# Four graph layers on one core: layer 2's first block moved ahead of W1, the residual row's store and load moved to the end of k, a smaller count for the weight ring, and VectorE in GpSimd's place for the deep weight sums

## The chip, the core and the metric

The kernel runs on one core of a Trainium2 chip. The metric is device time in microseconds (us), the median over runs of the same program. Before the change it is 2749.14 us, the median of three runs that span 2746.19 to 2756.6 us. One execution was profiled: it took 2744.72 us, and the span of its profile, from the first to the last instruction, is 2742.9 us.

The engines are named as the profile names them: PE is the matrix engine (TensorE), PEld its weight load, DVE is VectorE, ACT is ScalarE, POOL is GpSimd, SP is SyncE, which issues most transfers here. A queue is the in-order list of instructions of one engine.

## The reference, cut to what matters

The input is x of shape (128, 64, 512) in float32, that is 8192 rows of 512, with 128 graphs of 64 nodes and an adjacency matrix `adj` (64 x 64) for each. Four layers follow each other, each with a residual and a layer norm:

```
x = _layernorm(x + _L0_gnn_ref(x, adj, L0_gnn_W1, ...), axis=-1)     # relu(S x W1 + b1), norm, S h W2 + b2, + x
x = _layernorm(x + _L1_gnn_ref(x, adj, L1_gnn_w, L1_gnn_a), axis=-1) # tanh/exp scores, A x w
x = _layernorm(x + _L2_gnn_ref(x, adj, L2_gnn_W1, ...), axis=-1)     # three times adj (x W) + b, relu between
x = _layernorm(x + _L3_gnn_ref(x, nodemask, adj, adj, L3_gnn_W_qkv, L3_gnn_W_out, L3_gnn_b_out), axis=-1)  # 8 heads
```

S is a normalised incidence product made from `adj` (layer 0); layer 3 is attention over 64 nodes with a mask, to which 0.33 adj and 0.33 exp(-adj) are added after the softmax. All arithmetic is float32.

## The kernel before

**Tiles and groups.** Two graphs make a pair of 128 rows and four pairs a group of 512 rows, `xg`, a tile of 128 x 4 x 512 floats (1 MB). There are 16 groups, each taken through all four layers before its rows are written out. Three such x tiles exist (`xp`, three buffers), so group q's rows can be loaded only when group q - 3's rows have been stored.

**Products.** Every 512 x 512 weight product is made by `multiply` with seven quarter products in place of eight (a Strassen scheme: B11, T1, T2, B21, T3, B22, T4), PE accumulating in PSUM while ACT or DVE take the partial sums out. One quarter product of one left tile takes PE 1.73 us. The q, k and v products of groups 1 to 14 use the scheme twice over (`deep_multiply`): 42 stages of four or three 128 x 128 blocks, 0.89 or 0.67 us each, and the weights for them are sums made once, in group 0's time, and kept in DRAM (`deep_kept`). In these names `wqd`, `wkd`, `wvd` are the deep weight tiles.

**Deep weight sums.** `Weight.make_deep` makes them before the change. For each of w_q, w_k and w_v it takes the four quarters and the sums T1 to T4 that lie in weight ring tiles (`got`), lets POOL make 28 subtractions of 128 x 128 blocks (lines 335 to 338) into two `big` tiles, and stores everything from the POOL queue (lines 339 to 341). It is called from `Weight.making` (line 394), after POOL's own stores of T1 to T4 (line 392).

**The order of the work.** Three groups are in hand at once. In step s group s is in its first half ("a": layers 0 and 1), group s - 1 in its second half up to the scores ("b": layer 2, then q, k, the start of v), group s - 2 in its tail ("t": rest of v, softmax, output product, last norm). Each half is a Python generator that is cut at named points, and the list `order` (line 1905) says which piece is issued next; `step_1` and `step_last` replace it in the first and the last step. A steady step takes 165 to 172 us. In `order`, `t.v1 t.v2 a.c1 t.v a.w1a1 b.gt` means: two pieces of v of the tail group, then `a.c1` (`graph_T`: 128 small 64 x 64 products of x and S), the last of v, the first three quarter products of W1, then `b.gt` (the same kind of 128 small products, with `adj`, ahead of layer 2's first weight). From q to W1's end PE, DVE and ACT get their instructions in exactly this order (`strict`).

**The planner beside it.** Small work of DVE and ACT (norms, softmax, sums) is not at a fixed place: `Side` keeps a clock for PE, DVE and ACT from written-in costs and issues a task's next piece when it would not make its engine late. Tasks have ranks, the lower first. Layer 1's norm (`out_steps`, rank 3) and the last norm of the tail group (`ln3`, rank 2) run in q and k; the tail norm's remaining five pieces are 0.4 us of DVE and four scalings on ACT.

**Queues.** The build orders each queue itself: of the instructions that are ready in its model it takes the one that stands first in the program; `in_turn(E)` and `behind(key)` (both `tc.issue_after`) tie one instruction behind another of the same engine. On the chip an instruction waits only for the data and the buffers that it needs. That the order in SP's queue is not the order of the program shows in the `adn` loads: that of group 5 stands in step 4, before that step's `b.gh` (677.6 us in the trace), and was issued at 539.7 us, because its buffer was free.

**The weight ring.** Weight tiles (256 KB, deep ones 256 or 192 KB) pass through a ring of 16 buffers (`wring`, `RING`). `Stream.pump` writes the next loads into the program as long as the count of tiles held, `held`, stays within `RING`; `done` lowers the count after each product and pumps again.

**x, its store and its adds.** The store of a finished group is issued on SP by the last norm's steps when they are through (`then`, line 619, from line 1687). `load_x` (line 238) is a POOL-queue transfer that stands at `loadx`, after `b.k`, and waits for that store. Two rows are added to x by POOL-queue transfers that accumulate (`add_rows`, line 1075): gb3 from `shifted`, at `b.gh`, and bo after the softmax; the second is held back by a one-column copy on POOL, `due` (line 1667).

Of the kernel before, what the change touches and what calls it, by code (L numbers as in the profile page):

```python
# [8 lines left out]
FP = mybir.dt.float32  # L9
# [5 lines left out]
P = 128  # L15
# [20 lines left out]
B11, B21, B22, T1, T2, T3, T4 = range(7)  # L36
ORDER = (B11, T1, T2, B21, T3, B22, T4)
RING = 16

DEEP = ((B11, B21, T1, T2), (T3, T4, B22))  # L40
STAGES = (B11, B21, B22, T1, T2, T3, T4)
# [14 lines left out]
def kernel(  # L56
# [28 lines left out]
    nc = tc.nc  # L85
# [221 lines left out]
    class Weight:  # L307
# [15 lines left out]
            nc.sync.dma_start(out=t, in_=self.deep_kept[h][:, STAGES.index(s)].rearrange("p r n -> p (r n)"))  # L323
            return t.rearrange("p (r n) -> p r n", r=n)

        def make_deep(self, got):

            self.deep_kept = []
            for h, rs in enumerate(DEEP):
                n = len(rs)  # L330
                k = dram.tile([P, 7, n, P], FP, name=f"{self.name}deep{h}", tag=f"{self.name}deep{h}")
                d = big.tile([P, 4, n, P], FP, name=f"{self.name}deep_{h}", tag="big")
                for i, r in enumerate(rs):
                    b = got[r][0].rearrange("p k (n c) -> p k n c", n=2)
                    nc.gpsimd.tensor_sub(d[:, 0, i], b[:, 0, 1], b[:, 0, 0])
                    nc.gpsimd.tensor_sub(d[:, 1, i], b[:, 1, 1], d[:, 0, i])
                    nc.gpsimd.tensor_sub(d[:, 2, i], b[:, 1, 1], b[:, 0, 1])
                    nc.gpsimd.tensor_sub(d[:, 3, i], b[:, 1, 0], d[:, 1, i])
                    nc.gpsimd.dma_start(out=k[:, 0:2, i], in_=b[:, :, 0])
                    nc.gpsimd.dma_start(out=k[:, 2, i], in_=b[:, 1, 1])  # L340
                nc.gpsimd.dma_start(out=k[:, 3:7], in_=d)
                self.deep_kept.append(k)

        def load(self, q, what, u):
            t = self.tile(f"w{what}", q, u)
# [22 lines left out]
        def making(self, quads):  # L368


            got = [[None] * self.halves for _ in range(7)]
            to_keep = []
            for u, b in enumerate(quads):
                t1, t2, t3, t4 = (self.tile(f"t{n}", 0, u) for n in range(1, 5))
                vec.tensor_sub(t1, b[0, 1], b[0, 0])
                vec.tensor_sub(t2, b[1, 1], t1)
                if self.halves == 1:
                    yield
                vec.tensor_sub(t3, b[1, 1], b[0, 1])
                vec.tensor_sub(t4, b[1, 0], t2)  # L380
                made = {T1: t1, T2: t2, T3: t3, T4: t4}
                whole = {B11: b[0, 0], B21: b[1, 0], B22: b[1, 1]}
                kept = {}
                for what, t in (whole | made if self.scaled else made).items():
                    kept[what] = dram.tile([P, 2, Q], FP, name=f"{self.name}k{what}_{u}", tag=f"{self.name}k{what}_{u}")
                    to_keep.append((kept[what], t))
                self.kept.append(kept)
                for what, t in (whole | made).items():
                    got[what][u] = t
            with in_turn(POOL):  # L390
                for k, t in to_keep:
                    nc.gpsimd.dma_start(out=k, in_=t)
                if self.deep:
                    self.make_deep(got)
            yield got

        def load_raw(self):
# [50 lines left out]
    class Stream:  # L448


        def __init__(self, uses):
            self.todo = []
            for wt, q in uses:
                if wt.deep and 0 < q < NGRP - 1:
                    if wt is w_q:
                        trio = (w_q, w_k, w_v)
                        self.todo += [(trio[i // 2], q, (i % 2, s), 1) for i, s in deep_stages(6)]
                elif q == 0:
                    self.todo.append((wt, q, None, 8))
                elif (wt, q) == (w_o, NGRP - 1):  # L460
                    self.todo.append((wt, q, None, 4))
                else:
                    self.todo += [(wt, q, what, wt.halves) for what in ORDER]
            self.here = {}
            self.held = 0
            self.to_make = {}
            self.uses = uses

        def pump(self, uses=None):
            end = len(self.todo) - uses if uses else 0  # L470
            while len(self.todo) > end and self.held + self.todo[0][3] <= RING:
# [605 lines left out]
    def shifted(g, key):  # L1077

        with behind(key):
            if 0 < g["q"] < NGRP - 1:  # L1080
                add_rows(g["x"], gb3_bc)
            else:
                for p in range(G):
                    vec.tensor_add(g["x"][:, p, :], g["x"][:, p, :], gb3_bc)
            prepare_masks(g)
# [359 lines left out]
    def second_half(g):  # L1445
# [70 lines left out]
                    else:  # L1516
                        act.activation(o[:, :, h, :], cols, AF.Relu, bias=gb2_col[:, k : k + 1])  # L1517
        if not alone:
            shifted(g, f"l0w2_{q + 1}.u2")
        h2.sums()  # L1520
        if q == NGRP - 1:
            last_add["h2s"] = newest(DVE)
# [67 lines left out]
        else:  # L1590
# [1 line left out]
            side.start(1.5)  # L1592
            before = groups[q - 1]
            if "ln3" in before:
                before["ln3"] = side.add(before["ln3"], 2)
            more = side.add(left.more_sums(), 0)
            for _ in range(4):
                side.step(more)
# [63 lines left out]
        yield "soft2"  # L1662
        pts = [turn_probs(g, duo, probs[duo]) for duo in range(2)]
        if 0 < q:
            due = small.tile([P, 1], FP, name=f"due_{q}", tag="due")
            with in_turn(POOL):
                nc.gpsimd.tensor_copy(due, pts[0][0][:, 0, 0:1])
            with in_turn(POOL):
                add_rows(xg, bo_bc)
        yield "ptp"  # L1670
        left = Left(f"oT_{q}")
        taken(0, attend(g, 0, pts[0], v), left)
# [11 lines left out]
        whole(gen)  # L1684
        yield "o"
        o = out[q * T : (q + 1) * T, :].rearrange("(p t) d -> t p d", t=P)
        steps = norm_steps(xg, f"l3_{q}", lambda: nc.sync.dma_start(out=o, in_=xg), f"l2_{q + 1}")
        for _ in range(G + 2):
            next(steps)
        g["ln3"] = steps  # L1690
# [198 lines left out]
    def taken(duo, ps, left, both=False):  # L1889
# [25 lines left out]

    step_last = """
# [44 lines left out]
    with in_turn(SP):  # L1961
        load_adn(first)
        w_2.load_raw()
    scaling, bw_parts = w_2.scale(), w_2.beta_times()
    for n, (who, q, name) in enumerate(todo):
        if n == n_start:
# [113 lines left out]
```

## Time and profile before

| what | value |
|---|---|
| median of 3 runs | 2749.14 us |
| profiled execution, its span | 2744.72 us, 2742.9 us |
| PE busy | 2691.6 us, 98% |
| DVE, ACT, POOL busy | 76%, 45%, 6% |
| mean DMA rate | 183 GB/s |
| steady steps, from the start of one `xtp` transpose to the next (395.1 to 2576.3 us) | 165.4 to 171.6 us |
| store of x: issue to landing | 6.1 to 7.3 us, median 6.5 |
| load of x: issue to landing | 8.5 to 11.0 us, median 9.2 |

PE's idle time is what can be saved: 51 us of the span. The profile names for each wait the engine that ended it, or "issue" when the engine waited for nothing that the profile shows. Windows of the trace give busy time, the granted clock of PE (PEclk, 1.00 is full) and the share of the 16 DMA engines' time that packets took (1.00 and a little over is full).

### The profile page before, as it was taken

To read this page: it belongs to the slowest core of one execution; us is meant where nothing else is said; L and a number is where in the kernel's file an instruction comes from. 1 tells how busy PE (TensorE), PEld (TensorE's weight loads), DVE (VectorE), ACT (ScalarE), POOL (GpSimd) and SP (SyncE) were. 2 spreads that over 40 slices of the span, in tenths; PEclk is the share of its full clock that TensorE was granted. 3 is DMA by queue.
4 is the path that set the end of the run, shared out by engine and by line. 5 is a ranking of instruction groups with operands and counts; after the bars stand their busy time and mean duration, and the time that the engine had idled before them with its cause. 6 is when DMAs were issued, how large, how long until landed. Compare 5 with 4: busy or idle time off the path is not lost.

```text
span 2742.9 us, 74095 instructions
## 1 busy us (share of the span) xinstructions
PE 2691.6 (98%) x30536; PEld 2377.5 (87%) x30536; DVE 2092.4 (76%) x4169; ACT 1231.5 (45%) x2860; POOL 162.6 (6%) x259
## 2 busy tenths in 40 slices
PE   9998999999999999999999999999999999999998
PEld 8887888898898889889898888888988888898887
DVE  6777687686887868778687776877868787786866
ACT  3333335355362634526355363453634536264452
POOL 3019000000000000000000000000000000000000
PEclk9999999999999999999999999999999999999999
DMA  8446657576574756648575575665856658475652
GB/s 270 140 146 226 179 157 229 145 231 159 174 230 136 236 154 209 188 136 254 146 235 154 146 242 142 223 161 147 247 143 227 156 167 236 128 237 156 188 170 77
DMA packets 349518, 502.36 MB, mean 183 GB/s; under 512 B 63344, under 2 KB 196752, under 8 KB 348800
## 3 DMA queue, kind: packets, MB, share of 16 engines
q1 hardware_dynamic: 323072, 428.59, 50.2%
q0 software_dynamic: 25968, 68.92, 10.6%
q8 instruction: 243, 3.98, 0.6%
q14 instruction: 91, 0.75, 0.1%
q10 hardware_dynamic: 144, 0.13, 0.0%
HBM read 427.59 MB, written 40.57 MB: 171 GB/s over the span
## 4 chain that ended last, share of the span: by engine, by line
PE 91%; DVE 5%; ACT 2%; issue 1%; POOL 1%; DMA 0%; DVEq 0%; ACTq 0%; POOLq 0%
PE a_l0w L860 8%; PE a_l0w L145 7%; PE a_l2b L860 4%; PE a_l2c L860 4%; PE b_l0w L860 4%; PE a_wo L860 4%; PE a_v L145 4%; PE b_l0w L145 3%; PE a_l2a L145 3%; PE a_k L145 3%; PE a_q L145 3%; PE a_l1w L860 3%; PE gt_l0h L632 2%; PE gt_l L145 2%; PE c_l0w L860 2%; PE b_l2c L860 2%
## 5 line engine op out<-in xcount | busy, mean ns | idle before, releaser
L860 PE MATMUL a_l0w<-w2w,aT_l0h 128*128 128x256 f32 x720 | 164.3, 381 | 0.0
L860 PEld LDWEIGHTS a_l0w<-w2w,aT_l0h 128*128 128x128 f32 x720 | 135.6, 190 | 18.8
L145 ACT ACTIVATE sm<-sm,mx 128x64 f32<-128x64 f32 x416 | 139.1, 340 | 0.2
L1517 ACT ACTIVATE aT_h<-gth,gb_col 128x256 f32<-128x256 f32 x124 | 47.1, 490 | 159.0 <-PE gth L1505 159.0
L145 ACT COPY aT_l<-gt_l 128x512 f32<-128x512 f32 x124 | 64.4, 596 | 101.4 <-PE gt_l L145 101.4
L860 PE MATMUL b_l0w<-w2w,s_l0h 128*128 128x256 f32 x480 | 108.5, 379 | 0.0
L145 PE MATMUL a_v<-wvd,d_xT 128*128 128x128 f32 x700 | 95.4, 280 | 9.1 <-issue 7.0
L860 PEld LDWEIGHTS b_l0w<-w2w,s_l0h 128*128 128x128 f32 x480 | 91.1, 190 | 12.5
L145 PEld LDWEIGHTS a_v<-wvd,d_xT 128*128 128x128 f32 x700 | 85.9, 193 | 11.2 <-issue 7.1
L238 POOL DMA_DIRECT2D x<-in_x_dram x14 | 10.9, 777 | 1370.1 <-PE a_k L145 550.9
L145 PE MATMUL a_k<-d_xT,wkd 128*128 128x128 f32 x700 | 91.9, 275 | 0.0
L145 PE MATMUL a_q<-d_xT,wqd 128*128 128x128 f32 x700 | 91.9, 275 | 0.0
L145 ACT ACTIVATE x<-x,shift_l,rs_l 128x512 f32<-128x512 f32 x112 | 91.7, 819 | 0.0
L860 PE MATMUL a_l2b<-gwbw,aT_h 128*128 128x256 f32 x360 | 86.8, 383 | 2.4 <-ACT rs_h L573 2.4
L879 ACT COPY c_l2c<-a_l2c 128x512 f32<-128x512 f32 x16 | 9.1, 570 | 174.5 <-PE a_l2c L860 174.5
L145 PEld LDWEIGHTS a_q<-d_xT,wqd 128*128 128x128 f32 x700 | 85.9, 192 | 0.7
L860 PE MATMUL a_l1w<-ww,aT_l 128*128 128x256 f32 x360 | 85.1, 379 | 0.2 <-ACT aT_l L643 0.2
L860 PE MATMUL a_l2c<-gwcw,aT_h 128*128 128x256 f32 x360 | 85.2, 379 | 0.0
L145 PEld LDWEIGHTS a_k<-d_xT,wkd 128*128 128x128 f32 x700 | 84.9, 192 | 0.0
L583 DVE BATCH_NORM_STATS2 st_l<-x 128x6 f32<-128x512 f32 x128 | 82.4, 676 | 1.6
L914 DVE TENSOR_TENSOR x<-a_l0w,u_l0w 128x512 f32<-128x512 f32 x15 | 10.4, 691 | 94.8 <-PE a_l0w L860 94.8
L145 ACT ACTIVATION_READ_ACCUMULATOR sm<-sm,mx 128x1 f32 x416 | 80.2, 193 | 0.0
(678 smaller groups left out, 7350.8 us busy)
## 6 DMA issues: line engine op xcount, KB each, us to landing
w2w<-w2k SPq DMA_DIRECT2D x210, 256.0 KB, 2.8
wqd<-wqdeep SPq DMA_DIRECT2D x98, 256.0 KB, 2.8
wkd<-wkdeep SPq DMA_DIRECT2D x98, 256.0 KB, 2.8
wvd<-wvdeep SPq DMA_DIRECT2D x98, 256.0 KB, 5.8
wqd<-wqdeep SPq DMA_DIRECT2D x98, 192.0 KB, 2.5
wkd<-wkdeep SPq DMA_DIRECT2D x98, 192.0 KB, 3.5
wvd<-wvdeep SPq DMA_DIRECT2D x98, 192.0 KB, 7.1
w1aw<-w1ak SPq DMA_DIRECT2D x60, 256.0 KB, 6.1
```

The costliest lines, as they stand in the source:

```text
L145: return op(*args, **kwargs)
L238: g["load_x"] = lambda: (nc.gpsimd if q > 1 else nc.sync).dma_start(out=xg, in_=xsrc)
L583: vec.bn_stats(st, xg[:, p, :])
L632: ten.matmul(ps[g][f * C : (f + 1) * C, c, p, :], src(2 * duo + p)[rows, c0 : c0 + C], mat[rows, 2 * duo + p, :], start=True, stop=True,)
L860: ten.matmul(acc[:, blk, :], lhsT, rhs, start=(first and blk == 0 and i == 0), stop=(last and i == n_k - 1), skip_group_check=True,)
L879: last_add[f"{key}.{what}"] = (act.copy(t, ps) if res is None else vec.tensor_add(t, ps, res(m, n))).ins
L914: last_add[f"{key}.d"] = vec.tensor_add(dst(1, 1), pa, s5).ins
L1517: act.activation(o[:, :, h, :], cols, AF.Relu, bias=gb2_col[:, k : k + 1])
```

## The change

- In `order`, layer 2's first block (`b.gt`, and `b.l2a1`, `b.l2a`) goes ahead of layer 0's `a.c1` and W1 (`a.w1a1`, `a.w1a`): both pairs change places.
- The store of group q - 3 no longer follows its norm; it is issued at `loadx`, at the end of k, on SP behind what SP was given before, and the load of x stands in order on POOL. The tail norm's rank goes from 2 to 4, behind layer 1's norm.
- A cap takes the place of `RING` in `pump`: 9 from `ebb` (just before `loadx`) until `flow` (before `b.l2b1`), 16 otherwise. The ring keeps its 16 buffers.
- The gb3 add, like the bo add, waits on POOL for a `due` copy, here of a column of h2, which is made at `b.gh`.
- `make_deep` becomes a generator for one half of one weight. It loads the raw quarters again from DRAM on the POOL queue into a `big` tile, and at its next call DVE makes four subtractions (of 512 or 384 columns) in order, and POOL's queue stores the result. Its six calls are spread: deep0 to deep2 in step 1 during q, k and the scores of group 0, the rest in step 2.

```diff
+EBB = 9
...
-        def make_deep(self, got):
-
-            self.deep_kept = []
-            for h, rs in enumerate(DEEP):
...
-                for i, r in enumerate(rs):
-                    b = got[r][0].rearrange("p k (n c) -> p k n c", n=2)
-                    nc.gpsimd.tensor_sub(d[:, 0, i], b[:, 0, 1], b[:, 0, 0])
...
+        def make_deep(self, h):
+
+            rs = DEEP[h]
+            n = len(rs)
+            if h == 0:
+                self.deep_kept = []
+            k = dram.tile([P, 7, n, P], FP, name=f"{self.name}deep{h}", tag=f"{self.name}deep{h}")
+            b = big.tile([P, n, 2, 2, P], FP, name=f"{self.name}raw_{h}", tag="big")
+            for i, r in enumerate(rs):
+                if r < 3:
+                    src = self.quad_src(0, *((0, 0), (1, 0), (1, 1))[r])
+                else:
+                    src = self.kept[0][r]
+                nc.gpsimd.dma_start(out=b[:, i].rearrange("p k n c -> p k (n c)"), in_=src)
+            yield
+            d = big.tile([P, 4, n, P], FP, name=f"{self.name}deep_{h}", tag="big")
+            for m, l, r in (
+                (0, b[:, :, 0, 1], b[:, :, 0, 0]), (1, b[:, :, 1, 1], d[:, 0]),
+                (2, b[:, :, 1, 1], b[:, :, 0, 1]), (3, b[:, :, 1, 0], d[:, 1]),
+            ):
+                with in_turn(DVE):
+                    vec.tensor_sub(d[:, m], l, r)
+            for m in range(2):
+                nc.gpsimd.dma_start(out=k[:, m], in_=b[:, :, m, 0])
+            nc.gpsimd.dma_start(out=k[:, 2], in_=b[:, :, 1, 1])
+            nc.gpsimd.dma_start(out=k[:, 3:7], in_=d)
+            self.deep_kept.append(k)
+            yield
...
-                if self.deep:
-                    self.make_deep(got)
...
-            self.held = 0
+            self.held, self.cap = 0, RING
...
-            while len(self.todo) > end and self.held + self.todo[0][3] <= RING:
+            while len(self.todo) > end and self.held + self.todo[0][3] <= self.cap:
...
+    def add_rows_after(xg, row, key, what):
+
+        due = small.tile([P, 1], FP, name=f"due_{key}", tag="due")
+        with in_turn(POOL):
+            nc.gpsimd.tensor_copy(due, what)
+        with in_turn(POOL):
+            add_rows(xg, row)
...
-                add_rows(g["x"], gb3_bc)
+                add_rows_after(g["x"], gb3_bc, f"gb3_{g['q']}", what)
...
-            shifted(g, f"l0w2_{q + 1}.u2")
+            shifted(g, f"l0w2_{q + 1}.u2", h2.t[:, 0, 0:1])
...
-                before["ln3"] = side.add(before["ln3"], 2)
+                before["ln3"] = side.add(before["ln3"], 4)
...
-        steps = norm_steps(xg, f"l3_{q}", lambda: nc.sync.dma_start(out=o, in_=xg), f"l2_{q + 1}")
+        g["store"] = lambda: nc.sync.dma_start(out=o, in_=xg)
+        steps = norm_steps(xg, f"l3_{q}", g["store"] if q == NGRP - 3 else None, f"l2_{q + 1}")
...
     order = """
-        t.v1 t.v2 a.c1 t.v a.w1a1 b.gt t.soft a.w1a a.resid b.l2a1 b.l2a a.w1b1 t.soft2 t.ptp a.w1b t.pv a.lnh b.l2b1
-        t.osum a.c2a b.l2b a.c2b b.gb3 load a.w21 b.gh a.w2 rows b.l2c1 b.l2c2 a.ss a.den sumso t.o1 t.o2 b.l2c t.o3 a.c3 b.agg rows2 t.o
-        rows3 a.p1 b.xT t.ln3 a.p2 b.q1 a.ln1 b.q b.k1 b.k loadx b.v0 prep b.dots
+        t.v1 t.v2 b.gt t.v b.l2a1 deep3 a.c1 t.soft b.l2a a.w1a1 a.w1a deep4 a.resid a.w1b1 t.soft2 t.ptp a.w1b t.pv a.lnh flow b.l2b1
+        t.osum a.c2a b.l2b a.c2b deep5 b.gb3 load a.w21 b.gh a.w2 rows deep6 b.l2c1 b.l2c2 a.ss a.den sumso t.o1 t.o2 b.l2c t.o3 a.c3 b.agg rows2 t.o
+        rows3 a.p1 b.xT t.ln3 a.p2 b.q1 a.ln1 b.q b.k1 b.k ebb loadx b.v0 prep b.dots
     """.split()
...
-        a.c3 sumsq2 a.p1 b.xT sumsk a.p2 b.q1 a.ln1 b.q rows2 b.k1 b.k loadx b.v0 prep b.dots
+        a.c3 sumsq2 a.p1 b.xT sumsk a.p2 b.q1 a.ln1 b.q rows2 deep0 b.k1 deep1 b.k loadx b.v0 prep b.dots deep2
...
         elif who == "loadx":
             if q > 2 and "ln3" in groups[q - 3]:
                 side.finish(groups[q - 3]["ln3"])
-            groups[q]["load_x"]()
+                with in_turn(SP):
+                    groups[q - 3]["store"]()
+            with in_turn(POOL):
+                groups[q]["load_x"]()
...
+        elif who.startswith("deep"):
+            n = int(who[4:])
+            if q == (3 if n > 2 else 2):
+                if n > 0:
+                    next(deep_parts[n - 1])
+                if n < 6:
+                    deep_parts[n] = (w_q, w_k, w_v)[n // 2].make_deep(n % 2)
+                    next(deep_parts[n])
+        elif who in ("ebb", "flow"):
+            stream.cap = (RING, EBB)[who == "ebb"] if q > 2 else RING
+            stream.pump()
```

More of the change, by code (lines that the diff above doesn't have):

```diff
@@ L324, in load_deep @@
             return t.rearrange("p (r n) -> p r n", r=n)
-        def make_deep(self, got):
-            self.deep_kept = []
-            for h, rs in enumerate(DEEP):
-                n = len(rs)
-                k = dram.tile([P, 7, n, P], FP, name=f"{self.name}deep{h}", tag=f"{self.name}deep{h}")
-                d = big.tile([P, 4, n, P], FP, name=f"{self.name}deep_{h}", tag="big")
-                for i, r in enumerate(rs):
-                    b = got[r][0].rearrange("p k (n c) -> p k n c", n=2)
-                    nc.gpsimd.tensor_sub(d[:, 0, i], b[:, 0, 1], b[:, 0, 0])
[L336 to L342, printed above, removed]
+        def make_deep(self, h):
[25 more added lines that the diff above has]
+            yield
@@ L1075, in add_rows, with shifted @@
         nc.gpsimd.dma_start(out=xg, in_=row.unsqueeze(1).to_broadcast([P, G, D]), accum_op=ALU.add)
-    def shifted(g, key):
+    def add_rows_after(xg, row, key, what):
[4 more added lines that the diff above has]
+            add_rows(xg, row)
+    def shifted(g, key, what=None):
         with behind(key):
             if 0 < g["q"] < NGRP - 1:
-                add_rows(g["x"], gb3_bc)
+                add_rows_after(g["x"], gb3_bc, f"gb3_{g['q']}", what)
             else:
@@ L1664, in second_half @@
         if 0 < q:
[L1665 to L1669, printed above, removed]
+            add_rows_after(xg, bo_bc, f"bo_{q}", pts[0][0][:, 0, 0:1])
         yield "ptp"
@@ L1963 @@
         w_2.load_raw()
+    deep_parts = {}
     scaling, bw_parts = w_2.scale(), w_2.beta_times()
```

## The prediction

> **What bounds the kernel now.** I read the page first, its busy shares, slices and queues (packets, MB, share):
>
> ```profile
> PE 2691.6 (98%) x30536; PEld 2377.5 (87%) x30536; DVE 2092.4 (76%) x4169; ACT 1231.5 (45%) x2860; POOL 162.6 (6%) x259
> PE   9998999999999999999999999999999999999998
> POOL 3019000000000000000000000000000000000000
> q8 instruction: 243, 3.98, 0.6%
> ```
>
> PE is the bound. The change takes no PE work away, so it can only win idle time (51 us) and slow clock. POOL works in one slice, 206 to 274 us, in which PE is below 90%. Next, the view of PE's waits (total, times, longest):
>
> ```profile
> PE a_v L145 <- issue: 7.0, 3, 2.6
> PE dot L145 <- issue: 6.9, 5, 2.3
> PE gt_l L145 <- issue: 5.5, 5, 1.9
> PE a_k L860 <- DVE kT L914: 4.2, 1, 4.2
> PE a_v L145 <- ACT aT_l L145: 2.0, 1, 2.0
> PE c_v L145 <- issue: 1.0, 1, 1.0
> ```
>
> Five of these lines (7.0 + 6.9 + 5.5 + 2.0 + 1.0 = 22.4 us) lie in one place of the steady step, the tail's v, the scores (`dot`) and the next `gt_l<-smat,x`. What ends them is not data. The timeline shows two of them inside a run of equal instructions:
>
> ```profile
> 430.91 0.83 PE L145 MATMUL a_v<-wvd,d_xT 128*128 128x128 f32 x6
> 434.05 0.38 PE L145 MATMUL a_v<-wvd,d_xT 128*128 128x128 f32 x2 [2.31 <-issue]
> 436.53 1.84 PE L145 MATMUL gt_l<-smat,x 64*64 64x64 f32 x107
> 440.25 0.57 PE L145 MATMUL gt_l<-smat,x 64*64 64x64 f32 x21 [1.88 <-issue]
> ```
>
> PE's queue has 62318 records, and q8 brought 243 packets of 16 KB: one for 256. Counting the records, all 15 stops fall on a number with remainder 193 modulo 256. So PE waits there for its own instructions. In the trace the packet for the next 256 starts 1.1 to 5.1 us (mean 2.8) after PE entered the block before, takes 1.0 us, and PE goes on about 1.4 us later; in light DMA traffic it starts after 0.8 to 1.5 us. The windows of the same step show the traffic (busy by engine, then PEclk, DMA share, GB/s):
>
> ```profile
> 395.00:410.00 15.00, 14.88 (x127) 14.38 (x128) 13.72 (x28) 10.34 (x20) 0.00 (x0) 1.00 0.65 190
> 410.00:424.00 14.00, 14.00 (x128) 14.00 (x128) 12.34 (x26) 9.46 (x19) 0.76 (x1) 1.00 1.01 348
> 424.00:434.00 10.00, 7.74 (x190) 7.47 (x189) 6.87 (x12) 4.65 (x9) 0.00 (x0) 1.00 1.05 367
> 434.00:441.00 7.00, 5.08 (x150) 4.66 (x150) 3.01 (x5) 2.77 (x6) 0.00 (x0) 1.00 0.56 172
> 1774.60:1778.00 3.40, 3.16 (x51) 3.04 (x51) 1.75 (x3) 0.00 (x0) 0.00 (x0) 0.50 0.61 217
> 252.30:255.70 3.40, 3.40 (x39) 2.39 (x41) 0.00 (x0) 0.59 (x1) 3.36 (x8) 0.50 0.73 222
> ```
>
> From the store of x (409.4 us) the DMA engines are full until 434. The last two rows show a second price: after a long stop PE runs 3.4 us at half clock, which is 1.7 us lost. That happened four times in mid-run: after the stops of 4.2 us (251), 1.3 us (213), 2.35 us (1775) and 2.1 us (2111). Last, the timeline of DVE near 245 us, for the 4.2 us:
>
> ```profile
> 245.11 0.69 DVE L379 TENSOR_TENSOR wvt<-wvb,wvb 128x512 f32<-128x512 f32 x1 [2.68 <-DMA wkdeep<-wkt]
> 249.20 0.90 DVE L380 TENSOR_TENSOR wvt<-wvb,wvt 128x512 f32<-128x512 f32 x1 [3.39 <-DMA wkdeep<-wkt]
> ```
>
> DVE waits 6.1 us for ring buffers that POOL's sums still hold, and the add to kT that PE needs stands behind it.
>
> **The change, part by part.** *Deep sums off POOL.* What goes in 200 to 275 us: the 4.2 us wait and its half clock (two groups of matmuls took 3.78 for 1.89 and 2.47 for 2.10 us: 2.3); the 1.3 us wait of `xtp` for scalings on DVE that took 2.75 us for two beside POOL, and its half clock (1.7); 1.0 us at `a_q` and 0.4 at `a_l0w`, DVE being late: two-tensor subtractions took up to 0.94 us there and 0.69 elsewhere, POOL's own 0.89 and 0.45. Sum 10.9. What comes: 24 subtractions on DVE, 12 of 512 columns (0.69 us) and 12 of 384 (0.56), 15 us. Two sets (5.0 us) fall in step 1, where DVE is busy 11.8 of 12 us (228 to 240), and deep0's subtractions stand only three products (5.2 us) behind the issue of their four loads; a POOL-queue transfer of 256 KB lands after 2.8 to 11.1 us by its rows. Between nothing, if DVE has the time that POOL's contention took from it, and 8 (5.0 and a load 3 us late), I take 3. The other four sets (10 us) fall in step 2, where DVE is 46% to 93% busy; cover is PE's own products. Bounds 0 and 5 (deep5 and deep6 near layer 0's norm, 93%); I take 1. Part: -10.9 + 3 + 1 = -6.9; bounds -10.9 and +2.1. POOL's queue now carries 21 raw loads and 24 stores; x's load of step 2 stands half a step behind the last of them: 0.
>
> *Order of gt/l2a and c1/W1.* The two runs of 128 small matmuls and the two sets of seven products change places one for one, so PE's time and the small runs' places stay. Layer 1's norm must be through at `b.gt`: its last scaling on ACT starts 3.7 us after k ends, `b.gt` would start 10.4 after (the start of `gt_l<-smat,x` in steps without a stop). Softmax's ACT work now runs mainly beside W1, whose sums DVE takes, instead of beside l2a, whose copies ACT takes; a copy there ended 0.26 us ahead of PE (459.02 for 459.28). I take 0; bounds -1 and +6.5 (0.5 us in 13 steps).
>
> *Rank of the tail norm.* By the planner's costs its 0.4 us on DVE fits between layer 1's pieces of 0.67, and its last scaling still comes about 10 us before k ends. The store is then ready; 0.
>
> *Store and load of x.* The store moves from 14.3 us before k's end (409.4 for 423.7) to about 0.6 after, past 17 weight loads on SP. By the medians it lands at k + 7.1, the load (issued 0.6 after the landing, median 9.2) at k + 16.9. PE reads x at `a.c1`: 10.4 + 2.1 (`gt_l`) + 0.9 (last v stage) + 5.2 (three products) = k + 18.6. Margin 1.7 us. By the longest rows (7.3 and 11.0) x is 0.9 late; in 13 steps that is 0 to 12 us. I take 1. On POOL the bo copy is next in order and due 30 us later: 0.
>
> *The cap of 9.* I cost it at nothing and do not count on it. A load waits on the chip only for its ring buffer, and there are still 16; the `adn` rows show that SP's queue does not keep the program's order. If it does bind, see the third case.
>
> *Traffic.* The k stretch falls from 348 GB/s to the weights alone, and the v stretch gets the store and load. Eleven v stages free a buffer each, and each takes a 256 KB load: 2.9 MB and 2.1 MB of x, at 367 GB/s 13.6 us, so the DMA engines are full to about k + 14, as now to k + 10. But the backlog when the scores start (k + 4.3) is 5 loads and the store less what has drained, 1.3 + 1.05 - 1.58 = 0.8 MB, where before SP had its eight transfers of 256 KB (2 MB) out. Taking every one of the 15 stops with a packet start of 1.2 us instead of its own, 7.7 us of the 22.4 are left, 14.7 won; with half the backlog I take half, 7. One of two half clocks goes, 1.7. Bounds: 22.4 + 3.4 won; or 13 steps as bad as the worst one (4.2 us), 32 lost. The gb3 add leaves 449 to 459 us, where no stop lies, for the stretch behind `b.gh` (512 to 524 us, 125 GB/s); agg comes at about 552: 0.
>
> The Trainium skill, "Runtime: NRT & Kernel Launch", section "Instruction fetch mechanics", says that an engine fetches blocks of 256 instructions by its own DMA queue and that crossing a block is mostly hidden. The trace agrees on the block and not on the hiding; by the page the traffic part would be left out, and the sum would be -5.9, 2743. "SBUF — State Buffer", section "SBUF: two separate sides", speaks against the change: while DVE runs a two-port operation, POOL cannot write the descriptors of its transfers. By that the raw loads beside a busy DVE would come later still, at the upper bound of 8, and the sum would be -9.6, 2739.5; no row here shows it.
>
> Sum: -6.9 (deep sums) - 7 - 1.7 (traffic) + 1 (x) = -14.6. From 2744.7 that is 2730; the median of the runs shown lies 4.4 above the profiled execution, so 2734.5 us, 0.54% less.
>
> **The rivals.** *The burst only moves.* The v stretch is as full as before, the stops stay at 22.4; only the deep sums' 6.9 are won: 2742. For it: 5.0 MB in 13.6 us. Against it: the scores now meet a queue that has just begun to fill.
>
> *Relief in full.* The cap bites, no weights are loaded for eight stages, and store and load run alone: 14.7 + 3.4 + 10.9 = 29 won, 2720; with every stop gone 36.7, 2712.
>
> *x comes late.* The store meets a v stretch that asks for 256 KB in 0.78 us (336 GB/s), more than k's 290, so both transfers can be slower than their rows, and PE stops at `gt_l<-smat,x` in `a.c1`, in 13 steps. Each us beyond the margin costs 13. With the deep sums' -6.9 and nothing won on traffic, it makes the kernel slower by 0.5% (13.7 us) from 1.6 us beyond, x at k + 20.2. With 3 us beyond: +39 - 6.9, 2781. For it: the margin is 1.7 us. Against it: after v the weights ask only 150 GB/s.
>
> **How the numbers follow.** Changes under 0.5% (13.7 us) can't be told from none. Forecast 0.42 (own range 2724 to 2742: 0.26 faster, 0.16 same); burst moves 0.27 (0.04 and 0.23); relief 0.13 (faster); x late 0.18 (0.17 slower, 0.01 same). Faster 0.43, same 0.40, slower 0.17. The range goes from the relief case's end, 2712, to 2760, where it takes in small latenesses and leaves out 0.13 to 0.15 of x late and a few hundredths at the ends.
>
> **What would show it.** POOL's 9 in the fourth slice gone and no wait of `a_k` for kT; the store issued within 1 us of k's end and x landed by k + 18; no `gt_l<-smat,x` that waits for a DMA; fewer "issue" stops at `dot` and v. I am wrong if the stops grow or move to `ptp` or `gt_l0h`, if `gt_l<-smat,x` waits each step, or if DVE waits for raw loads in 230 to 300 us.

## The result and the profile after

The changed kernel takes 2766.82 us (median of four runs, 2764.19 to 2769.34); the kernel before, run beside it, took 2748.54 us. The ratio is 1.0061, with a 95% interval of 1.0038 to 1.0085: **0.6% slower**, where 0.54% faster was forecast. The profiled execution has a span of 2766.8 us, 23.9 more than before.

From the page of the changed kernel, its busy times and POOL's slices:

```profile
PE 2708.2 (98%) x30536; PEld 2386.0 (86%) x30536; DVE 2090.5 (76%) x4193; ACT 1235.0 (45%) x2860; POOL 120.4 (4%) x186
POOL 2003200000000000000000000000000000000000
```

POOL's 9 in the fourth slice is gone, as forecast. But PE is *busy* 16.6 us longer with the same 30536 matmuls; 12.0 us of that is time at half clock, as shown below. The view of PE's waits (total, times, longest) has the rest:

```profile
PE gt_l L146 <- issue: 8.3, 6, 2.8
PE dot L146 <- issue: 7.8, 3, 2.7
PE a_v L146 <- issue: 7.7, 3, 4.0
PE b_v L146 <- issue: 3.0, 1, 3.0
PE a_k L870 <- DVE kT L924: 2.6, 1, 2.6
PE a_l2a L146 <- DVE aT_h L146: 2.5, 11, 0.2
PE b_l2a L146 <- issue: 1.9, 1, 1.9
PE c_v L146 <- issue: 1.5, 1, 1.5
```

The lines that end in "issue" are the stops at the edges of PE's 256-instruction blocks, as before, only longer: up to 4.0 us. Counted over the whole kernel (idle time of PE over 0.3 us at a record number within three of 193 modulo 256, which takes in one at l2b that the prediction left out), they grew from 24.6 to 33.8 us. The longest one, in the timeline of PE:

```profile
1448.49 2.10 PE L146 MATMUL gt_l<-atc,x 64*64 64x64 f32 x128
1450.51 0.71 PE L146 MATMUL a_v<-wvd,d_xT 128*128 128x128 f32 x4
1455.18 0.59 PE L146 MATMUL a_v<-wvd,d_xT 128*128 128x128 f32 x2 [3.96 <-issue]
```

PE entered this block at 1448.55 and was through it 2.7 us later; the packet with the next 256 instructions started 4.2 us after the entry, took 0.9 us, and PE went on 1.6 us after that. The windows of that step (k ends at 1438.1; busy by engine, then PEclk, DMA share, GB/s) show what the DMA engines did meanwhile, and what came after the stop:

```profile
1424.00:1438.50 14.50, 14.50 (x132) 14.50 (x131) 12.76 (x26) 9.80 (x19) 0.00 (x0) 1.00 0.92 286
1438.50:1449.00 10.50, 10.50 (x241) 10.10 (x243) 8.71 (x15) 6.04 (x12) 0.78 (x1) 1.00 0.99 339
1449.00:1456.00 7.00, 3.04 (x118) 2.80 (x109) 1.85 (x3) 2.32 (x6) 0.00 (x0) 0.88 0.84 293
1456.00:1467.00 11.00, 11.00 (x158) 9.16 (x157) 6.68 (x11) 4.18 (x7) 0.00 (x0) 0.76 0.35 99
```

k is relieved, but the nearly full stretch now reaches to 1454, across the scores, the end of v and layer 2's first small matmuls. After the stop PE ran two periods at half clock (6.8 us in the last two windows). In mid-run, PE had 17 us of half clock before and 41 us after, 8.5 and 20.5 us lost. SP's queue in the same place shows the cap of 9:

```profile
1439.33 0.39 SPq L1701 DMA_DIRECT2D out_dram<-x  x1
1439.81 0.46 SPq L360 DMA_DIRECT2D gwaw<-in_gW_dram  x1
1440.36 1.36 SPq L362 DMA_DIRECT2D gwaw<-gwak  x1
1441.82 1.43 SPq L360 DMA_DIRECT2D w1aw<-in_W1T_dram  x1
1443.34 1.38 SPq L362 DMA_DIRECT2D w1aw<-w1ak  x2
```

It holds nothing: weight loads follow the store at once. Built with a cap of 16 in place of 9, the program has the same list of instructions for every engine.

So the difference in span is +9.2 us of stops, +12.0 us of half clock and 2.5 us of a new wait at `a_l2a`, less some 4 us won at the head. The 4 us that are left are not waits: from the first to the last end of k, PE's busy time outside half clock grew from 2152.8 to 2156.6 us. The kernels below that have the new order without the move of x show it too (e2 2158.8, e3 2157.7), so it goes with the order; why was not traced.

### The profile page after: what moved, and what is told of

The parts are those of the page before. It is cut to its first block, busy times and chain, and to the rows that moved or that the text cites. A ratio compares the mean times of both kernels' runs of the same rounds, so it can differ in the third digit from the quotient of the medians.

```text
span 2766.8 us, 74110 instructions
## 1 busy us (share of the span) xinstructions
PE 2708.2 (98%) x30536; PEld 2386.0 (86%) x30536; DVE 2090.5 (76%) x4193; ACT 1235.0 (45%) x2860; POOL 120.4 (4%) x186
## 4 chain that ended last, share of the span: by engine, by line
PE 88%; DVE 5%; issue 3%; ACT 3%; DMA 0%; POOL 0%; DVEq 0%; POOLq 0%; ACTq 0%
PE a_l0w L870 8%; PE a_l0w L146 7%; PE a_l2b L870 4%; PE b_l0w L870 4%; PE a_v L146 4%; PE a_l2c L870 4%; PE a_wo L870 4%; PE b_l0w L146 3%; PE a_k L146 3%; PE a_q L146 3%; PE a_l2a L146 3%; PE a_l1w L870 3%; PE gt_l0h L642 2%; PE c_l0w L870 2%; PE b_l2b L870 2%
## 5 line engine op out<-in xcount | busy, mean ns | idle before, releaser
L146 PE MATMUL a_l2a<-aT_l,gwaw 128*128 128x256 f32 x312 | 78.2, 395 | 2.5 <-DVE aT_h L146 2.5
L146 PE MATMUL a_l0w<-w1aw,aT_l 128*128 128x256 f32 x336 | 80.5, 382 | 0.0
```

Source lines behind the costliest of these rows:

```text
L146: return op(*args, **kwargs)
```

## The experiments

The first theory, **traffic**: the moved store and load of x make PE's instruction packets late. Its rivals: the new **order** does it, the **deep** sums on VectorE do it, and, later, **luck** with the place of the block edges. All times are medians; "stops" are counted as above, "half clock" is the time lost to it in mid-run, both in the profiled execution, which is one run of several: those of e7 and e9 lie 5 and 8 us below their medians, those of e6 and e13 6 and 4 above. The last column counts, to within two, the short blocks (under 7 us of PE's own work, 410 to 2600 us) that had a transfer of x, a copy or a row add in flight one to three us after PE entered them.

| kernel | us | before beside it | ratio, 95% | stops, us | half clock, us | beside |
|---|---|---|---|---|---|---|
| before | 2748.54 | | 1 | 24.6 | 8.5 | 9 |
| changed | 2766.82 | 2748.54 | 1.0061 [1.0038, 1.0085] | 33.8 | 20.5 | 32 |
| e1 deep alone | 2740.74 | 2747.72 | 0.9971 [0.9961, 0.9981] | 22.4 | 12.0 | 10 |
| e2 order alone | 2748.18 | 2747.72 | 1.0003 [0.9993, 1.0013] | 16.7 | 10.2 | 13 |
| e3 x as before | 2736.83 | 2747.72 | 0.9966 [0.9953, 0.9980] | 15.7 | 5.1 | 12 |
| e4 deep as before | 2793.51 | 2747.72 | 1.0167 [1.0151, 1.0184] | 38.7 | 27.3 | 33 |
| e5 quarter of x | 2745.32 | 2749.17 | 0.9987 [0.9977, 0.9997] | 18.4 | 8.5 | 29 |
| e6 two copies | 2764.42 | 2749.17 | 1.0053 [1.0036, 1.0071] | 38.0 | 15.4 | 36 |
| e7 x on SP | 2765.09 | 2749.17 | 1.0055 [1.0036, 1.0074] | 30.0 | 13.7 | 33 |
| e8 later sums | 2739.26 | 2749.17 | 0.9964 [0.9953, 0.9976] | 19.0 | 5.1 | 12 |
| e9 real hold | 2768.04 | 2751.45 | 1.0067 [1.0050, 1.0084] | 25.4 | 13.7 | 34 |
| e10 copies late | 2740.57 | 2751.45 | 0.9965 [0.9950, 0.9980] | 18.2 | 5.1 | 14 |
| e11 shifted | 2765.44 | 2751.45 | 1.0054 [1.0039, 1.0068] | 17.8 | 5.1 | 12 |
| e12 sums spread | 2736.72 | 2751.45 | 0.9953 [0.9940, 0.9966] | 17.3 | 3.4 | 11 |
| e13 before, half a block | 2762.05 | 2747.09 | 1.0043 [1.0028, 1.0058] | 29.6 | 15.3 | 10 |
| e14 changed, half a block | 2780.55 | 2747.09 | 1.0107 [1.0085, 1.0130] | 36.5 | 23.9 | 32 |
| e15 x as before, half a block | 2751.12 | 2747.09 | 1.0017 [1.0002, 1.0033] | 21.4 | 3.4 | 11 |

### One part at a time: e1 to e4

e1 has the new `make_deep` and its six calls in the old order:

```diff
-        t.v1 t.v2 a.c1 t.v a.w1a1 b.gt t.soft a.w1a a.resid b.l2a1 b.l2a a.w1b1 t.soft2 t.ptp a.w1b t.pv a.lnh b.l2b1
+        t.v1 t.v2 a.c1 t.v a.w1a1 deep3 b.gt t.soft a.w1a deep4 a.resid b.l2a1 b.l2a a.w1b1 t.soft2 t.ptp a.w1b t.pv a.lnh b.l2b1
```

> The kernel before with the deep sums made by VectorE and nothing else. Three theories of the 18 us that the change lost. Traffic: the store and load of x, moved to the end of k, meet the weights of v, so that PE's instruction packets come later in the scores, v and gt. Order: layer 2's first block ahead of W1 does it, by its own waits and by which instructions stand at the edges of the 256-instruction blocks. Deep: the sums on VectorE do it. Traffic and order expect here the 6.9 us that I gave this part: 2739 to 2744 us, PE's stops for instructions as before (22 us in the v, scores and gt part), no wait of a_k for kT. Deep expects 2755 us or more.

Measured 2740.74, 7.0 us less. The wait of `a_k` for kT did not go: it is 2.4 us (4.2 before).

e2 has only the new order and the `due` copy for gb3:

```diff
-        t.v1 t.v2 a.c1 t.v a.w1a1 b.gt t.soft a.w1a a.resid b.l2a1 b.l2a a.w1b1 t.soft2 t.ptp a.w1b t.pv a.lnh b.l2b1
+        t.v1 t.v2 b.gt t.v b.l2a1 a.c1 t.soft b.l2a a.w1a1 a.w1a a.resid a.w1b1 t.soft2 t.ptp a.w1b t.pv a.lnh b.l2b1
```

> The kernel before with the new order of the step (gt and l2a ahead of c1 and W1, and the add of gb3 held to gh) and nothing else; x is stored and loaded where it was. Traffic expects 2748 to 2753 us: the 11 waits of a_l2a for aT_h (2.5 us) and stops for instructions of 20 to 25 us, at most 6 periods of half clock. Order expects 2760 to 2775 us, stops of 30 us or more and 8 or more periods of half clock.

Measured 2748.18, ratio 1.0003: no difference. The stops fell by 7.9 us. Waits of `a_l2a` (2.8 us), a longer wait of `a_k` for kT (6.1 us, 4.2 before) and 6.0 us more of PE's busy time outside half clock took it back.

e3 is the changed kernel without the move of x:

```diff
-                before["ln3"] = side.add(before["ln3"], 4)
+                before["ln3"] = side.add(before["ln3"], 2)
...
-        g["store"] = lambda: nc.sync.dma_start(out=o, in_=xg)
-        steps = norm_steps(xg, f"l3_{q}", g["store"] if q == NGRP - 3 else None, f"l2_{q + 1}")
+        steps = norm_steps(xg, f"l3_{q}", lambda: nc.sync.dma_start(out=o, in_=xg), f"l2_{q + 1}")
...
-                with in_turn(SP):
-                    groups[q - 3]["store"]()
-            with in_turn(POOL):
-                groups[q]["load_x"]()
+            groups[q]["load_x"]()
```

> The changed kernel with the store and load of x put back (stored at the end of the tail's norm, rank 2, loaded when the store has landed). Traffic expects the loss gone: 2740 to 2747 us, stops of 20 to 25 us, at most 6 periods of half clock. Order expects 2760 us or more, as the changed kernel.

Measured 2736.83, 0.34% *faster* than before. Order and deep theories are out: moving x costs 30 us by the medians, 26 by the ratios to the kernel before beside each, 32 by the profiled spans. PE's waits in e3:

```profile
PE a_v L146 <- issue: 3.9, 3, 2.4
PE a_l2a L146 <- DVE aT_h L146: 3.0, 13, 0.2
PE a_k L870 <- DVE kT L924: 2.7, 1, 2.7
PE dot L146 <- issue: 2.1, 3, 0.9
PE gt_l L146 <- issue: 1.8, 2, 1.2
```

and its windows at the same step (k ends at 1423.0), in answer to the four above:

```profile
1409.00:1423.00 14.00, 14.00 (x128) 14.00 (x127) 12.71 (x26) 9.37 (x18) 0.78 (x1) 1.00 1.02 360
1423.00:1433.50 10.50, 10.50 (x217) 10.10 (x217) 8.28 (x15) 6.06 (x12) 0.00 (x0) 1.00 1.05 366
1433.50:1440.50 7.00, 4.63 (x144) 4.28 (x144) 3.32 (x6) 3.01 (x6) 0.00 (x0) 1.00 0.51 149
1440.50:1451.50 11.00, 11.00 (x169) 9.29 (x167) 8.05 (x14) 7.96 (x24) 0.00 (x0) 1.00 0.43 127
```

The DMA engines are no less full in the first two windows; in the third they have 149 GB/s to move, not 293. PE's list of instructions is the same in both kernels, so the same matmuls stand at the edges. From e3 to the changed kernel the stops rise by 18.1 us and the half clock by 15.4, together 33.5, and the span by 32.0: that is the whole price.

e4 is the changed kernel with `make_deep` as before (the edit is the removed and added function of the change, turned round).

> The changed kernel with the deep sums back on GpSimd. Traffic and order expect 2770 to 2775 us (the changed kernel's 2767 and the 4 to 7 us that the deep sums won), the wait of a_k for kT of about 4 us back, the stops for instructions unchanged at about 32 us. Deep expects about 2748 us.

Measured 2793.51, some 20 us above what traffic and order expected and 45 above what deep did. The timeline of PE names the cause:

```profile
290.62 3.69 PE L633 MATMUL gt_l<-smat,x 64*64 64x64 f32 x128 [13.46 <-DMA x<-in_x_dram]
```

and that of POOL the reason:

```profile
281.91 0.54 POOL L342 DMA_DIRECT2D wvdeep<-wvdeep  x1
282.43 0.78 POOL L239 DMA_DIRECT2D x<-in_x_dram  x1
```

The change also ties the load of x to its turn on POOL. With the old sums the load of step 1 stands behind all of them and is issued at 282.4 us (247.5 in the changed kernel), so PE waits 13.5 us and then runs 13.7 us at half clock. The deep sums are worth 7 us alone and 27 us once the load of x stands in turn behind them.

### What about the move costs: e5 to e7, e9, e10

e5 keeps the two transfers in their place and cuts them to a quarter:

```diff
+            n_ld = 1 if q > 3 else G
...
+        n_st = 1 if 0 < q < NGRP - 3 else G
-        g["store"] = lambda: nc.sync.dma_start(out=o, in_=xg)
+        g["store"] = lambda: nc.sync.dma_start(out=o[:, 0:n_st], in_=xg[:, 0:n_st])
```

> The changed kernel, but from group 4 on only one quarter of x is loaded (GpSimd fills the rest with ones) and in the same steps only a quarter of the tail's rows is stored: the same two transfers at the same place with 0.5 MB instead of 2.1 MB, and most of the output left out. Theory traffic (bytes beside the weights of v make PE's instruction packets late): stops for instructions fall from 33.8 to 15-22 us, half clock from 10 periods in mid-run to 2-5, time 2736 to 2746 us. Rival place (the wait for the store, GpSimd's writing of descriptors or the queue position does it, whatever the size): 2758 to 2768 us, stops of 30 us.

Measured 2745.32, stops 18.4: "place" is out, bytes count. A quarter of them still costs a little: the profiled span is 6.1 us above e3's, with 2.7 us more of stops and 3.4 of half clock.

e6 leaves x where it was before and adds two transfers nobody needs:

```diff
+            if q > 2 and "ln3" in groups[q - 3]:
+                s1, s2 = (dram.tile([P, G, D], FP, name=f"copy{n}_{q}", tag=f"copy{n}") for n in range(2))
+                with in_turn(SP):
+                    nc.sync.dma_start(out=s1, in_=x[q * T : (q + 1) * T, :].rearrange("(p t) d -> t p d", t=P))
+                with in_turn(POOL):
+                    nc.gpsimd.dma_start(out=s2, in_=s1)
```

> The kernel with x stored and loaded as before (2736.8 us) and two copies of 1 MB between DRAM tensors that nobody reads, issued where the changed kernel issues the store and the load of x, the second waiting for the first. No work of the kernel depends on them. Traffic: stops for instructions rise from 15.7 to 27 us or more, 6 or more periods of half clock, 2755 to 2770 us. Rival (PE's time was lost because its data, x, came at another time): 2735 to 2742 us, stops as in the kernel without the copies.

Measured 2764.42: against e3 28 us, nearly the whole loss, without touching anything that PE depends on. Its waits of PE:

```profile
PE gt_l L146 <- issue: 13.6, 12, 2.5
PE a_v L146 <- issue: 6.8, 3, 3.1
PE dot L146 <- issue: 5.7, 4, 2.2
PE b_v L146 <- issue: 2.7, 1, 2.7
```

e10 issues the same two copies some 67 us before the end of k, before l2c (`rows copies deep6 b.l2c1`).

> The kernel with x as before and the two copies of 1 MB that nobody reads, now issued before l2c, where PE runs long runs of 128x256 matmuls and the trace shows 125 to 190 GB/s. Traffic beside small matmuls and a high demand for weights is the theory: here the copies cost 0 to 6 us, 2737 to 2743 us, stops for instructions of 15 to 19 us. If it is the bytes alone, wherever they come: 2755 to 2770 us as with the copies at the end of k.

Measured 2740.57, ratio 0.9965 where e3 had 0.9966: no cost by the ratios, 4 us by the medians, where e6 had 28. The windows of the copies and of the zone after k:

```profile
1361.00:1375.00 14.00, 14.00 (x67) 12.32 (x66) 12.81 (x36) 4.74 (x8) 0.55 (x1) 1.00 0.88 283
1438.50:1445.50 7.00, 5.18 (x146) 4.75 (x140) 3.87 (x7) 3.36 (x7) 0.00 (x0) 1.00 0.54 176
```

In the first PE is busy for all of the 14 us with 67 long matmuls: a block lasts long enough there for a late packet. The DMA share is 0.88 there, so e10 alone does not part long blocks from lighter traffic; the counts at the end of this document do.

e7 and e9 ask if holding the weights back helps. e7 puts the load of x on SP, so that what stands behind it waits for the store:

```diff
-            g["load_x"] = lambda: (nc.gpsimd if q > 1 else nc.sync).dma_start(out=xg, in_=xsrc)
+            g["load_x"] = lambda: (nc.gpsimd if q == 2 else nc.sync).dma_start(out=xg, in_=xsrc)
...
-            with in_turn(POOL):
+            with in_turn(POOL if q < 3 else SP):
                 groups[q]["load_x"]()
```

> The changed kernel with the load of x issued by SP, three weight loads behind the store, in place of GpSimd: SP waits there until the store has landed and the loads of W1 behind it are really held, which the cap of 9 did not do. Traffic: the store drains beside three loads only, so the stops at the scores and v shrink; x and the held loads then come together beside gt and l2a: stops of 18 to 27 us, 2742 to 2757 us. If only GpSimd's queue was at fault: 2735 to 2742 us. If holding the weights does not help: 2762 us or more.

Measured 2765.09, above what traffic expected. But the hold was short. The load of x was issued 3.1 us after the weight load before it, and stops are 30.0:

```profile
1440.34 1.32 SPq L360 DMA_DIRECT2D w1aw<-in_W1T_dram  x1
1443.47 0.37 SPq L239 DMA_DIRECT2D x<-in_x_dram  x1
```

e9 makes the cap bind by an element that ACT writes into each tile first:

```diff
+        def gate(self, to):
+            if self.cap < RING and self.mark is not None:
+                act.copy(to, self.mark)
...
             t = self.tile(f"w{what}", q, u)
+            stream.gate(t[:, 0, 0:1])
...
                 act.copy(t, ps)
+                stream.mark = t[:, 0, 0:1]
```

> The changed kernel with the cap of 9 made to bind: under the cap each weight load has to wait for an element that ACT writes into its tile out of the newest copy of a finished product, so SP has nothing to issue but the store for about eight stages of v and scores. ACT gets some 20 copies of one column more in a step. Theory traffic: store and load run with few weights beside them, stops for instructions fall from 33.8 to 22 us or less, half clock to 5 periods or fewer, 2737 to 2750 us. If the held loads only form a new burst beside gt and l2a: 2758 us or more, stops of 30 us. If PE then waits for weights: waits that end with a DMA, above 2770 us.

Measured 2768.04, like the changed kernel. This time the hold is real. SP's queue:

```profile
1429.16 0.52 SPq L364 DMA_DIRECT2D gwaw<-gwak  x1
1429.84 0.39 SPq L1711 DMA_DIRECT2D out_dram<-x  x1
1438.13 0.38 SPq L362 DMA_DIRECT2D gwaw<-in_gW_dram  x1
1438.82 0.33 SPq L364 DMA_DIRECT2D gwaw<-gwak  x1
1439.26 0.48 SPq L362 DMA_DIRECT2D w1aw<-in_W1T_dram  x1
```

and PE in the same step:

```profile
1439.49 2.10 PE L146 MATMUL gt_l<-atc,x 64*64 64x64 f32 x128
1441.52 0.38 PE L146 MATMUL a_v<-wvd,d_xT 128*128 128x128 f32 x1
1445.02 1.23 PE L146 MATMUL a_v<-wvd,d_xT 128*128 128x128 f32 x5 [3.12 <-issue]
```

For 9 us no weight load is issued; then x's load (issued at 1437.0) and three released loads start together, and the packet of the block entered at 1439.5 starts 3.0 us late. The transfers of x still lie beside 34 short blocks. The stops are less (25.4 us) and the profiled span is 9 us below that of the changed kernel, but the medians show no gain, and some small new waits came with it (`a_l0w` for DVE, 12 of 0.2 us). What part of the stops the hold takes off in a usual run stays open.

### Luck with the edges: e11, e13 to e15

e11 puts 64 one-column matmuls into e3, right behind the first matmul. They write into `full`, a PSUM tile that this first one sets up. No instruction is left out, but part of the output differs; why was not traced.

> The kernel with x as before and 64 matmuls of one column ahead of everything (128 records of PE, half a block), so that the edges of the instruction blocks fall on other matmuls in every step. If the 11 us won are a property of the order: 2734 to 2743 us, stops of 13 to 22 us. If they are luck with the edges: 2745 us or more, stops of 24 us or more.

It told nothing on luck. A float32 matmul is two MATMUL and two LDWEIGHTS records, so 64 of them are a whole block, and 240 of 242 edges fell on the same matmul as in e3. What it gives is a repeat: stops 17.8 for 15.7. Its time is longer because PE spent 27.3 us on the 128 records at the head.

e13 to e15 shift the edges by half a block, in the three kernels that matter:

```diff
+    for _ in range(32):
+        nc.tensor.matmul(full[0:C, 0:C], ones[0:C, 0:C], ones[0:C, 0:C], start=True, stop=True)
     nc.tensor.matmul(full, ones, ones[:, 0:1].to_broadcast([P, T]), start=True, stop=True)
```

> The kernel before with 32 small matmuls (64x64) ahead of everything: 64 MATMUL and 64 LDWEIGHTS records, half a block, so that every edge of the instruction blocks falls on another matmul. They cost PE about 1 us, beside a wait. If the stops belong to the order and its traffic, not to where the edges fall: within 8 us of the kernel before, stops for instructions of 17 to 32 us. If the edges decide: off by more than 8 us.

> The changed kernel with the same 32 small matmuls ahead. Moving x is the cause wherever the edges fall: slower than the kernel with x as before and the same 32 matmuls by 20 to 40 us, stops of 26 us or more, 6 or more periods of half clock in mid-run. If the changed kernel only had bad luck with the edges: within 8 us of the kernel with x as before, stops below 22 us.

> The kernel with x as before (new order, deep sums on VectorE) with the same 32 small matmuls ahead. If its 0.34% belong to the order: ratio 0.993 to 0.999 to the kernel before, stops of 12 to 23 us. If they were luck: 1.000 or more.

Measured 2762.05, 2780.55 and 2751.12. The expectation of e14 held: moving x costs 29.4 us here and 30.0 with the edges where they were, so it is no luck. Those of e13 and e15 missed, as all three kernels are 14 to 15 us slower. The 32 matmuls account for 5.3 of it (`gt_l<-smat,x` of group 0 starts at 11.65 us where it started at 6.39); I had priced them at 1. The other 9 us are put down to the other edges, by what the profiled executions show: the stops are 2.7 to 5.7 us longer, and with the 5.3 us and the change in half clock that makes 17.1 of the 21.8 us that e13's span grew, 11.4 of 11.1 in e14 and 9.3 of 10.9 in e15. The rest of e13 was not traced. The order and the deep sums together still win 11 us against e13.

### A version that beats both: e8, e12

In e3 the 2.7 us wait of `a_k` is left: DVE stands at a raw load of the deep sums with kT's add behind it. e8 moves the first set's sums behind k (`b.k1 b.k deep1` for `b.k1 deep1 b.k`).

> x as before, the new order, and the first set of deep sums moved behind layer 3's k of step 1, so that DVE no longer stands 2.5 us at a raw load with kT's add behind it. From the 2736.8 us of the kernel with x as before: the 2.7 us wait of a_k for kT goes and the 6.8 us of half clock after it (3.4 us): 2731 us (2727 to 2735). If another wait takes its place (sps, or the deep loads of q later in step 2): 2735 to 2740 us.

Measured 2739.26, no better than e3. The wait took another place: DVE stood 4.6 us at the second set's raw load, softmax's subtraction stood behind it, ACT's exponentials behind that, and a PSUM copy that PE needs behind those. From the timeline of PE in e8:

```profile
257.11 3.59 PE L870 MATMUL a_v<-wvt,d_xT 128*128 128x256 f32 x8 [4.20 <-ACT u_v L889]
```

e12 also gives every later set one place more:

```diff
-        t.v1 t.v2 b.gt t.v b.l2a1 deep3 a.c1 t.soft b.l2a a.w1a1 a.w1a deep4 a.resid a.w1b1 t.soft2 t.ptp a.w1b t.pv a.lnh flow b.l2b1
+        t.v1 t.v2 b.gt deep2 t.v b.l2a1 a.c1 t.soft b.l2a a.w1a1 a.w1a deep3 a.resid a.w1b1 t.soft2 t.ptp a.w1b deep4 t.pv a.lnh flow b.l2b1
```

> x as before, the new order, and the deep sums one place later from the second set on (the first set's sums behind k of step 1, the second's behind gt of step 2, then each next set at the place of the one after it), so that DVE stands at no raw load. Against the 2739.3 us with only the first set moved, the 4.2 us wait of a_v for u_v and 1.7 us of half clock go: 2733 us (2729 to 2737). If a raw load is late again at another place: 2738 to 2744 us.

Measured 2736.72, ratio 0.9953 [0.9940, 0.9966]: 0.47% faster than the kernel before and, by the ratios, 1.1% faster than the changed one. Both waits of step 1 are gone; 1.8 us came at `gt_l0h` in their stead. Its interval overlaps e3's, so only "x as before, with the new order and the deep sums on VectorE" is shown to be better, not this spread of them.

## Why the prediction was wrong, by its own steps

**Deep sums off POOL, -6.9: right.** e1 measured -7.0. Three details were not: one of VectorE's weight subtractions beside POOL took 1.44 us (231.36 us in the trace before), where I had read 0.94 as the most; the wait of `a_k` for kT stayed at 2.4 to 2.7 us (this is the 3 us that I took for step 1, a raw load that comes late), and I put the load of x in step 2 "behind the last of them: 0", but did not see that the change puts the load in POOL's turn, which makes the old and the new sums differ by 27 us (e4).

**Order of gt/l2a and c1/W1, 0: right in its number by luck** (e2, 1.0003, within the bounds of -1 to +6.5). It is the sum of things I had not priced: 7.9 us less of stops, against about 5 us of longer waits for DVE and 6.0 us more of PE's busy time, which I had said would stay.

**Rank of the tail norm, 0, and the cap of 9, 0: right.** The store was ready: it was issued 0.5 to 1.2 us after k in the steady steps. No load was held. In e9, where a hold does bind, the median shows no gain either, so "relief in full", the rival that needed the cap, had the wrong reason as well as the wrong size.

**Store and load of x, +1: right.** The store landed at k + 7.0 to k + 9.0 (I had 7.1), x at k + 14.7 to k + 17.8 (16.9), and `gt_l<-smat,x` began at k + 18.4 to k + 25.5 (18.6), never waiting for a DMA in the steady steps. The rival "x comes late" did not happen; that the time came nearest to it is no credit to it.

**Traffic, -7 and -1.7: wrong in sign.** This is the step that failed. It said that the backlog when the scores start, at k + 4.3, is 0.8 MB where it had been 2 MB, and took half the stops as won. Counted in one way for both kernels (bytes that SP and POOL have issued, less the bytes of packets that have ended, mean of the 13 steady steps), it is 1.5 MB in the changed kernel and 1.1 before: there was no relief to share out. Two slips made it look like one. My sum began with an empty queue, where 0.66 MB are out at k's end (0.66, and 1.11 of loads and 1.05 of the store, less 1.35 moved, is the 1.5). And I set bytes still to move against transfers not yet landed: eight whole transfers are 2 MB, of which about half had moved. After that I asked no more, though I wrote that the engines are "full to about k + 14, as now to k + 10". From k + 8 to k + 16, 1.2 MB are out where it had been 0.4, because the load of x comes when the store lands, beside the weights. But the short blocks reach to k + 20. Against e3 the term measured +18.1 us of stops and +15.4 us of half clock. Fewer stops were real, but they came with the order (e2, 7.9 us), in which I had put the small runs' places as unchanged.

**The bound was there.** "13 steps as bad as the worst one (4.2 us), 32 lost" stood among the bounds of this term; I let the range stop at 2760, and none of my rivals had the stops grow. (2734.5 is 0.53% less than 2749.14, not the 0.54 that I wrote.)

The Trainium skill, "Runtime: NRT & Kernel Launch", section "Instruction fetch mechanics", says that crossing a block is mostly hidden. The runs say when: over the 17 traces, between 410 and 2600 us, 2398 blocks held 7 us or more of PE's work and four of them ended in a stop (4.0 us in all); 986 were shorter and 254 of those did (395 us).

## What to carry to other kernels

Ask of a transfer that is moved what PE runs while it is in flight, not only whether it lands in time: beside long matmuls 2 MB more cost 0 to 4 us (e10), beside runs of small ones, which use up a block of 256 instructions in some 5 us, the same bytes cost 28 us (e6). A count kept while a program is written held nothing on the chip here; look in the queue's timeline whether anything was held. And any edit that changes the number of PE's instructions moves all block edges, with which some 9 us went here (e13 to e15): compare variants at the same edges before crediting one with 0.3%.

## What was not expected of the hardware

Stops grow with what the queues have out. Of the 986 short blocks, by MB issued and not yet moved when PE enters the block (counted as above; a copy from DRAM to DRAM counts once):

| MB out | blocks | stops over 0.3 us | mean stop, us |
|---|---|---|---|
| under 0.5 | 476 | 40 | 0.10 |
| 0.5 to 1 | 146 | 50 | 0.52 |
| 1 to 1.5 | 282 | 117 | 0.60 |
| 1.5 and more | 82 | 47 | 1.27 |

Of the 2398 longer blocks, 251 were entered with 1 MB or more out, and two of them ended in a stop. So in these traces it takes both, bytes out and a short block.

A packet of 16 KB is late although it is small beside either transfer; why it has to wait for the others was not tried.

A short stop is charged twice, but not by a fixed rule. In the changed kernel every block-edge stop of 1.9 us or more in the steady steps was followed by 3.4 us at half clock (6.8 after the one of 4.0) and none of 1.8 us or less; before, only two of the six stops of 2 us or more were.

A float32 matmul of one column took 0.43 us of PE at the head (27.3 us for 64 calls), and one of 64x64 with nothing beside it 0.22 us (7.09 us for 32), where the 64 calls of `gt_l` in a row take 2.10 us in mid-run. The difference was not followed up.
